# Two-layer graph network on one core: where the first two blocks' row sums are formed, and which engine copies the last values out of PSUM

## The chip, the cores and the metric

The kernel runs on 1 core of one Trainium2 chip. Five engines work side by side, each through its own instructions in order: PE (TensorE, matmuls), DVE (VectorE), ACT (ScalarE), POOL (GpSimd) and SP (SyncE, which here only issues DMAs). The metric is device time in microseconds (us) of one launch; smaller is better.

## What is computed

The reference has two graph-attention layers over N = 4096 nodes with F = 512 features, H = 4 heads of D = 128, all in float32. Cut to what matters here, layer 0 begins like this:

```
h   = relu(layernorm(x))                          # 4096 x 512
Xw  = per head: h_head @ W[head]                  # values, 4096 x 128
f1, f2 = Xw . V[head]                             # two scores for each node
sig = sigmoid(f1[i] + f2[j])                      # per head, 4096 x 4096
att = softmax over j of (adj * sig), where adj != 0
Xa  = att @ Xw                                    # encoder attention
Xn  = batchnorm(Xa) ... MLP ... decoder attention with the same att ... MLP
```

Layer 1 is a second attention of the same kind with other scores. The softmax's denominator is the sum over j of the unnormalised weights; this sum is what the change is about, together with the copying of `Xw`.

## The kernel before, in words

**First phase (L465 to L550).** The nodes are taken in eight blocks `ib` of 512, each of four groups `c` of 128 nodes. For a group, DVE (for the last `c` POOL) normalises the rows (`hn`, L507), PE transposes them (L519), and ACT takes the relu out of PSUM into `hT` (L520). Then, for each of the four groups and for each pair of heads `k`, PE multiplies by the values' weights (L537, 130 columns for each head: 128 values and two scores), ACT copies the 128 values of each head into the large tile `R` (L539), and DVE copies the scores (L540). A PSUM tile holds two heads; the pool `psum` has seven such banks. Meanwhile POOL issues eight DMAs (`copy_adjacency`, L481) that turn the float32 adjacency into bytes, `masks`, in DRAM. The rows of scores go through DRAM (`store_rows`, L189) and come back spread over all partitions (`rowb`).

**Encoder attention (`attention`, L221 to L442).** It runs over eight blocks `n`, each one head and one half of the targets (2048 columns). A block has 32 steps `j`, one for 128 sources. A step makes one weight tile `e` of 128x2048 (`tanh_weights`, L448): ACT computes a tanh (L450) and an exp (L451), DVE multiplies by the mask `a` (L452). PE multiplies the values with the tile into four PSUM banks (L371; for steps 0 and 1 the fourth bank comes later, L368). Every tile must also enter the denominator, and there are three ways:

- by DVE, which adds the tile to `acc` (L392 for the first two tiles of a block, then L394);
- *moved*: POOL issues two DMAs (L386), each for half a tile, that add it to a second sum;
- *by ones*: the tile is held and PE multiplies it with a matrix of ones into the bank `den` (`add_to_den`, L259 to L263). At a block's end the accumulated tiles go into `den` the same way.

The tuples in L62 to L64 say, for each block, which steps are moved and which are by ones: `ENC_FIRST` for block 0, `ENC_SECOND` for block 1, `ENC` for blocks 2 to 7. All steps that are named in neither are added by DVE.

Weight tiles come from eight buffers: two with the tag `ek` (`EP`), six with the name `e`. Mask tiles come from five buffers (`mask_tile`), loaded on SP's queue (L210). Every fifth tile is also kept in DRAM for the decoder by a DMA that ACT issues three steps later (L358). A block's denominators travel at fixed steps of the next block: DVE copies `den` (L268), POOL stores it and loads it as a column (L269, L274), DVE inverts it (L278, L279), POOL stores and spreads it (L282, L287), DVE scales and takes statistics (L561, L564). The raw products are copied out of PSUM by DVE (L557).

The order of instructions on each engine is a scheduler's at build time; `tc.issue_after` (also inside `pinned`) puts chosen instructions behind others on their own engine.

Of the kernel before, what the change touches and what calls it, by code (L numbers as in the profile page):

```python
# [39 lines left out]
N, F, H, D, P = 4096, 512, 4, 128, 128  # L40
IB = 512
NIB = N // IB
# [16 lines left out]
G_MAX = 75.0  # L59


ENC_FIRST = (), (6, 7, 14, 15, 22, 23, 30, 31)  # L62
ENC_SECOND = (13, 15, 17, 20, 22, 25), (5, 6, 10, 11, 30, 31)
ENC = (0, 2, 5, 7, 10, 12, 15, 17, 20, 22, 25), (8, 9, 30, 31)  # L64

GAT_FIRST = (0, 2, 4, 6, 8, 10, 12, 14, 16, 18, 20, 22, 24), (30, 31)
# [19 lines left out]
def kernel(ctx, tc, x, xT, adjT, w0, w0T, v0, wencT, wdecT, vecs, w1, w1T, a1, outT):  # L86
    nc = tc.nc
# [7 lines left out]
    R = [big.tile([P, N], FP, name=f"R{i}") for i in range(5)]  # L95
# [6 lines left out]
    def block(r, j):  # L102
        return r[:, j * D:(j + 1) * D]

    def bank():
        return psum.tile([P, IB], FP, name="ps")

    def bank1():
        return psum1.tile([P, IB], FP, name="den")
# [32 lines left out]
    def scores_of(j, k):  # L142

        return score[:, :, j // (NJ // NTB), 2 * k:2 * k + 2, j % (NJ // NTB)].rearrange("p s h -> p h s")
# [24 lines left out]
    def rsqrt(dst, var, eps):  # L169
        nc.vector.tensor_scalar_add(dst, var, eps)  # L170
        nc.scalar.activation(dst, dst, AF.Sqrt)
        return nc.vector.reciprocal(dst, dst)
# [12 lines left out]
    def heads_of(pv):  # L185

        return pv[:, 0:2 * DX].rearrange("p (h x) -> p h x", x=DX)

    def store_rows(dst, src, queue=nc.scalar):  # L189

        n = src.shape[-1]
        pr = bank()
        nc.tensor.transpose(pr[0:n, 0:P], src, ident)
        fr = consts.tile([P, P], FP, name="fr")
        nc.vector.tensor_copy(fr[0:n, :], pr[0:n, 0:P])
        queue.dma_start(dst.rearrange("h (q p) -> (h q) p", p=P), fr[0:n, :])

    def targets(tb):
        return score[:, 0, tb].rearrange("p h q -> p (h q)")

    def load_row(rowb, d, row):

        return nc.sync.dma_start(rowb, everywhere(d, row, 0, TB))

    def mask_tile(keep):
        return keep.tile([P, TB], U8, name="a", bufs=5)

    def load_mask(a, tb, j):

        return nc.sync.dma_start(a, masks[tb][j // MG][(j % MG) * P:(j % MG + 1) * P, :])  # L210

    @contextmanager
    def pinned(behind):

        with ExitStack() as stack:
            for i in behind:
                stack.enter_context(tc.issue_after(i.ins))
            yield
# [238 lines left out]
    with tc.tile_pool(name="keep", bufs=1) as keep:  # L457

        with tc.tile_pool(name="f_small", bufs=1) as small, tc.tile_pool(name="f_work", bufs=2) as work:
# [18 lines left out]
            def copy_adjacency(n, behind):  # L478

                t, g = divmod(n, NJ // MG)  # L480
                cast = nc.gpsimd.dma_start(masks[t][g], adjT[g * MG * P:(g + 1) * MG * P, t * TB:(t + 1) * TB])  # L481
                tc.add_manual_dep(cast.ins, behind.ins.name,
                                  mybir.DependencyInfo(mybir.DependencyClass.Sync, mybir.DependencyReason.DATA),
                                  reason="others first")

            for ib in range(NIB):
                st = work.tile([P, C, 6], FP, name="st")
                mv = work.tile([P, C, 2], FP, name="mv")
                rstd = work.tile([P, C], FP, name="rstd")

                def deviations(lo, hi):

                    with pinned([first_hn] if ib == 1 or lo == 1 else []):
                        for c in range(lo, hi):
                            nc.vector.bn_stats(st[:, c, :], xs[ib][:, c, :])
                    for c in range(lo, hi):
                        nc.vector.bn_aggr(mv[:, c, :], st[:, c, :])
                    return rsqrt(rstd[:, lo:hi], mv[:, lo:hi, 1], LN_EPS)

                last_dve = deviations(0, 1 if ib == 0 else C)  # L500
                hT = work.tile([P, C, IB], FP, name="hT")
                for c in range(C):
                    if ib == 0 and c == 1:
                        last_dve = deviations(1, C)
                    by_pool = c == C - 1
                    hn = work.tile([P, F], FP, name="hn", tag="hnp" if by_pool else "hn")
                    made = (nc.gpsimd if by_pool else nc.vector).tensor_scalar(  # L507
                        hn, xs[ib][:, c, :], mv[:, c, 0:1], rstd[:, c:c + 1], ALU.subtract, ALU.mult)
                    if ib == 0 and not by_pool:
                        first_hn = made  # L510

                    if by_pool and ib > 0:
                        with tc.issue_after(made.ins):
                            copy_adjacency(ib - 1, half_loaded)
                            if ib == NIB - 1:
                                copy_adjacency(ib, half_loaded)
                    pt = bank().rearrange("p (f n) -> p f n", n=P)
                    for fb in range(C):
                        last_pe = nc.tensor.transpose(pt[:, fb, :], hn[:, fb * P:(fb + 1) * P], ident)  # L519
                    last_act = nc.scalar.activation(hT[:, :, c * P:(c + 1) * P], pt, AF.Relu)  # L520
                if ib == 0:

                    pw = bank1()
                    with tc.issue_after(last_pe.ins):
                        for h in range(H):
                            nc.tensor.matmul(pw[:, 2 * h:2 * h + 2], w0Ts[:, h, :], v0s[:, h, :],
                                             start=True, stop=True)
                    pwh = pw[:, 0:2 * H].rearrange("p (h s) -> p h s", s=2)
                    with tc.issue_after(last_dve.ins):
                        nc.vector.tensor_copy(w0x[:, :, D], pwh[:, :, 0])  # L530
                        nc.vector.tensor_scalar_mul(w0x[:, :, D + 1], pwh[:, :, 1], 0.5)
                for c in range(C):
                    j = ib * C + c
                    for k in range(2):
                        pv = heads_of(bank())
                        for h in range(2):
                            nc.tensor.matmul(pv[:, h, :], hT[:, 2 * k + h, c * P:(c + 1) * P], w0x[:, 2 * k + h, :],  # L537
                                             start=True, stop=True)
                            nc.scalar.copy(block(R[2 * k + h], j), pv[:, h, 0:D])  # L539
                        nc.vector.tensor_copy(scores_of(j, k), pv[:, :, D:DX])  # L540
                if ib == SB - 1:
                    store_rows(rows[0], targets(0))
                    row0 = keep.tile([P, TB], FP, name="rowb", bufs=2)
                    row0_load = load_row(row0, rows[0], 0)
                    with tc.issue_after(row0_load.ins):
                        masks0 = []
                        for j in range(5):
                            a = mask_tile(keep)
                            masks0.append((a, load_mask(a, 0, j)))
# [45 lines left out]
        with tc.tile_pool(name="enc", bufs=1) as spool:  # L595

            with tc.issue_after(last_act.ins), tc.issue_after(masks0[-1][1].ins):
                attention("enc", keep, spool, tanh_weights, R[0:4], lambda h, tb: (rows[tb], h), out_enc,
                          (scaled, statistics), 6, lambda n: (ENC_FIRST, ENC_SECOND, ENC)[min(n, 2)],
                          (TINY, ALU.max), "write", row0=row0, masks0=masks0,  # L600
# [46 lines left out]
        with tc.tile_pool(name="m_small", bufs=1) as small, tc.tile_pool(name="m_work", bufs=3) as work:  # L647
# [10 lines left out]
            for h in range(H):  # L658
# [8 lines left out]
                for ib in range(NIB):  # L667
                    pv = bank().rearrange("p (c d) -> p c d", d=D)
# [40 lines left out]
    with tc.tile_pool(name="l_small", bufs=1) as small, tc.tile_pool(name="l_work", bufs=2) as work:  # L709
# [41 lines left out]
        for fb in range(C):  # L751
            with tc.issue_after(last_pe.ins):
                for h in range(H):
                    k = 2 * (fb * H + h)
# [64 lines left out]
        for ib in range(NIB):  # L819
            for c in range(C):  # L820
# [9 lines left out]
                j = ib * C + c  # L830
                r = rstd[:, c:c + 1]
                pvs, pvs_last = ahead.pop(0) if ahead else values(hT, c)
                for k in range(2):
                    pv = heads_of(pvs[k])
# [143 lines left out]
```

## Time and profile before

| what | us |
|---|---|
| median of 3 runs | 3267.72 (3262.49 to 3267.79) |
| the profiled execution's own time | 3260.23 |
| its span, first to last instruction | 3258.4 |
| PE busy | 3197.5 (98%) |
| DVE busy | 2665.4 (82%) |
| ACT busy | 2601.8 (80%) |
| POOL busy | 477.6 (15%) |

Times inside an execution are counted from the span's start. A row of a group of instructions gives the line, the engine, what it writes and reads, the count, the busy time and the mean of one in ns, then the idle time before it and what ended that. A matmul's record is longer than its share of PE: in float32 each product appears twice in the records, and they overlap. In a stretch without idle time (128 records of L371 in 55.48 us from 253.66 us on) one record takes 0.43 us of PE, and the eight of a step 3.43 us.

The stages, read from the trace: the first phase to about 69 us; encoder block 0 with its first weights at 65 us, block 1 from about 189, block 2 from about 317 (by ACT's work), and the last encoder work at about 1058; then an MLP, the decoder attention, a second MLP, and layer 1.

### The profile page before, as it was taken

How to read it: one execution, taken by the hardware profiler on the slowest of the kernel's cores; microseconds unless marked ns; L12 is line 12 of the kernel's file. 1: busy time of each engine (PE TensorE's matmuls, PEld its weight loads, DVE VectorE, ACT ScalarE, POOL GpSimd, SP SyncE). 2: the span in 40 equal slices, each digit the busy share in tenths (PEclk: the TensorE clock that was granted, in tenths of full speed). 3: DMA queues.
4: the chain of work that ended last, by engine and by line, in shares of the span. 5: the costliest groups of instructions: out<-in, count | busy, mean ns of one | idle time of the engine just before them, and what ended most of it. 6: DMA issues, size and time to landing. Idle time of an engine off the chain costs nothing.

```text
span 3258.4 us, 26085 instructions
## 1 busy us (share of the span) xinstructions
PE 3197.5 (98%) x8723; PEld 1484.0 (46%) x8723; DVE 2665.4 (82%) x1933; ACT 2601.8 (80%) x1908; POOL 477.6 (15%) x622
## 2 busy tenths in 40 slices
PE   7999999999999999999999999999999999999999
PEld 6334434444443464444444444448644444444443
DVE  6999999999999675556655565585599999999998
ACT  7999999999997459899999999566765666666664
POOL 2001221211211000000000000025412222122221
PEclk9999999999999999999999999999999999999999
DMA  9997988988986014434443443231488999889995
GB/s 208 196 195 226 259 227 230 266 224 226 268 232 177 4 64 130 147 127 129 153 142 125 139 153 122 78 121 56 129 207 216 218 229 243 214 210 238 218 214 143
DMA packets 211150, 578.48 MB, mean 178 GB/s; under 512 B 25068, under 2 KB 28172, under 8 KB 195016
## 3 DMA queue, kind: packets, MB, share of 16 engines
q0 software_dynamic: 67968, 222.51, 36.0%
q1 hardware_dynamic: 126432, 293.72, 27.1%
q10 hardware_dynamic: 16616, 60.60, 4.8%
q8 instruction: 68, 1.11, 0.1%
q14 instruction: 66, 0.54, 0.0%
HBM read 377.10 MB, written 84.29 MB: 142 GB/s over the span
## 4 chain that ended last, share of the span: by engine, by line
PE 68%; ACT 12%; DVE 9%; issue 7%; DMA 3%; POOL 0%; ACTq 0%; DVEq 0%; POOLq 0%
PE ps L371 52%; ACT e L450 7%; PE ps L613 7%; DVE e L452 5%; ACT e L451 4%; PE ps L809 3%; DMA a<-mask 2%; DVE acc L394 2%; PE den L262 1%; DVE e L904 1%; DVE R L394 1%; PE ps L670 1%; DMA acc<-e 1%; PE ps L368 1%; PE ps L537 1%
## 5 line engine op out<-in xcount | busy, mean ns | idle before, releaser
L371 PE MATMUL ps<-e,R 128*128 128x512 f32 x6024 | 2614.1, 594 | 37.5 <-DVE e L452 35.2
L371 PEld LDWEIGHTS ps<-e,R 128*128 128x128 f32 x6024 | 1140.1, 190 | 1504.8 <-issue 1396.6
L452 DVE TENSOR_TENSOR e<-e,a 128x2048 f32<-128x2048 f32 (+1 forms) x470 | 1051.7, 2259 | 383.7 <-ACT e L451 369.4
L450 ACT ACTIVATE e<-rowb,score 128x2048 f32<-128x2048 f32 (+1 forms) x470 | 912.4, 1968 | 85.9 <-PE ps L371 43.9
L451 ACT ACTIVATE e<-e 128x2048 f32<-128x2048 f32 (+1 forms) x470 | 870.6, 1879 | 6.1
L903 ACT ACTIVATE e<-rowb,nq,jcol 128x2048 f32<-128x2048 f32 x224 | 461.4, 2090 | 273.7 <-DMA w<-e 133.9
L904 DVE SCALAR_TENSOR_TENSOR e<-e,jcol,a 128x2048 f32<-128x2048 f32 (+1 forms) x265 | 591.8, 2267 | 7.3 <-ACT e L903 7.3
L394 DVE TENSOR_TENSOR acc<-acc,e 128x2048 f32<-128x2048 f32 x130 | 297.1, 2286 | 2.1
L394 DVE TENSOR_TENSOR R<-R,e 128x2048 f32<-128x2048 f32 x123 | 280.5, 2281 | 0.0
L386 POOL DMA_DIRECT2D w<-e x178 | 150.3, 847 | 613.4 <-DMA w<-e 356.1
L613 PE MATMUL ps<-R,w 128*128 128x512 f32 x512 | 220.3, 592 | 0.6 <-DVE w L571 0.6
L386 POOL DMA_DIRECT2D acc<-e x144 | 120.4, 881 | 542.9 <-DMA acc<-e 196.8
L287 POOL DMA_DIRECT2D rb<-rinvs x60 | 34.5, 580 | 1059.2 <-DVE R L561 865.9
L613 PEld LDWEIGHTS ps<-R,w 128*128 128x128 f32 x512 | 97.2, 190 | 122.7 <-issue 117.7
L634 ACT ACTIVATE ex<-ps,bias 128x512 f32<-128x512 f32 x64 | 44.0, 687 | 98.8 <-PE ps L613 79.0
L809 PE MATMUL ps<-w1x,hT 128*128 128x260 f32 x512 | 115.5, 384 | 1.4 <-ACT hT L787 1.4
L809 PEld LDWEIGHTS ps<-w1x,hT 128*128 128x128 f32 x512 | 96.5, 190 | 19.9 <-issue 3.3
L903 ACT ACTIVATE e<-w,nq,jcol 128x2048 f32<-128x2048 f32 (+1 forms) x41 | 67.4, 1711 | 24.5 <-DMA R<-e 24.4
L636 DVE SCALAR_TENSOR_TENSOR ex<-ex,re 128x512 f32<-128x512 f32 x64 | 45.0, 702 | 36.4 <-ACT re L635 36.2
L846 POOL TENSOR_TENSOR vacc<-vacc,R 128x128 f32<-128x128 f32 x120 | 65.8, 576 | 45.3 <-ACT R L839 45.0
L839 ACT ACTIVATE R<-ps,rstd 128x128 f32<-128x128 f32 x128 | 38.5, 371 | 29.3 <-PE ps L809 25.6
L262 PE MATMUL den<-e,ones 128*32 128x512 f32 x424 | 51.1, 598 | 0.0
(172 smaller groups left out, 1246.2 us busy)
## 6 DMA issues: line engine op xcount, KB each, us to landing
a<-mask SPq DMA_DIRECT2D x720, 256.0 KB, 4.1
w<-e POOLq DMA_DIRECT2D x178, 512.0 KB, 6.8
acc<-e POOLq DMA_DIRECT2D x144, 512.0 KB, 6.7
ekeep<-e ACTq DMA_DIRECT2D x48, 1024.0 KB, 7.6
e<-ekeep SPq DMA_DIRECT2D x48, 1024.0 KB, 4.9
mask<-in_adjT POOLq DMA_DIRECT2D x8, 2048.0 KB, 99.4
rowb<-rows SPq DMA_DIRECT2D x16, 1024.0 KB, 7.7
rb<-rinvs POOLq DMA_DIRECT2D x60, 256.0 KB, 4.2
```

The costliest lines, as they stand in the source:

```text
L262: last_ones = nc.tensor.matmul(den[s * 32:(s + 1) * 32, :], ones[:, 0:32], t[:, s * IB:(s + 1) * IB], start=start, stop=stop)
L371: last_main = nc.tensor.matmul(b, block(values[h], j), e[:, s * IB:(s + 1) * IB], start=(j == 0), stop=(j == NJ - 1))
L386: nc.gpsimd.dma_start(into_half, e_half, **({"accum_op": ALU.add} if j > moved[0] else {}))
L394: nc.vector.tensor_add(acc, acc, e)
L450: nc.scalar.activation(e, rowb, AF.Tanh, bias=column(score[:, 1], j, h), scale=0.5)
L451: last_act = nc.scalar.activation(e, e, AF.Exp, scale=0.5)
L452: last_dve = nc.vector.tensor_mul(e, e, a)
L613: last = nc.tensor.matmul(z, w[:, fb, o * P:(o + 1) * P], nodes(src[fb], ib), start=(fb == 0), stop=(fb == C - 1))
L809: m = nc.tensor.matmul(banks[k][:, 0:2 * DX], hT[:, fb, c * P:(c + 1) * P], w1x[:, fb, 2 * k:2 * k + 2, :].rearrange("p h x -> p (h x)"), ...
L846: nc.gpsimd.tensor_add(vacc[:, h, :], vacc[:, h, :], block(v1[h], j))
L903: last_act = nc.scalar.activation(e, rowb, AF.Relu, bias=column(nq, j, h), scale=column(jcol, j, h))
L904: last_dve = nc.vector.scalar_tensor_tensor(e, e, column(jcol2, j, h), a, ALU.add, ALU.mult)
```

## The change

Blocks 0 and 1 each take two more steps by ones. In block 0 the eight steps in four pairs become ten in five pairs, so the pairs also lie at other steps; in block 1 the pair 23, 24 is added. In the first phase the copies of values that ACT made for the last block of nodes (`ib` 7, both heads of a pair: 16 copies) and for the second head of each pair in the block before it (`ib` 6: 8 copies) are made by DVE. Nothing else is touched; the result is the same sum.

```diff
-ENC_FIRST = (), (6, 7, 14, 15, 22, 23, 30, 31)
-ENC_SECOND = (13, 15, 17, 20, 22, 25), (5, 6, 10, 11, 30, 31)
+ENC_FIRST = (), (5, 6, 11, 12, 17, 18, 24, 25, 30, 31)
+ENC_SECOND = (13, 15, 17, 20, 22, 25), (5, 6, 10, 11, 23, 24, 30, 31)
...
                         for h in range(2):
                             nc.tensor.matmul(pv[:, h, :], hT[:, 2 * k + h, c * P:(c + 1) * P], w0x[:, 2 * k + h, :],
                                              start=True, stop=True)
-                            nc.scalar.copy(block(R[2 * k + h], j), pv[:, h, 0:D])
+
+                            by_dve = ib + h >= NIB - 1
+                            (nc.vector.tensor_copy if by_dve else nc.scalar.copy)(block(R[2 * k + h], j), pv[:, h, 0:D])
                         nc.vector.tensor_copy(scores_of(j, k), pv[:, :, D:DX])
```

## The prediction

> **What bounds the kernel now.** The page says PE 98%, but its note says that a busy PE is not at its peak. So I read the waits of ACT alone, from the first weights (64 us) to the start of block 2 (330 us):
>
> ```profile
> engine line waited for: us in total, times, longest us
> ACT e L450 <- DVE e L452: 3.8, 1, 3.8
> ACT e L450 <- DMA acc<-e: 3.2, 1, 3.2
> ACT e L450 <- PE den L262: 1.8, 1, 1.8
> ```
>
> ACT waits three times in 266 us, 8.75 us in all, never in block 0's own steps. Where ACT does not wait, it sets the pace itself. The next view, groups by form between 81 and 330 us, gives the rates (count, busy us, mean ns, idle before):
>
> ```profile
> L452 DVE TENSOR_TENSOR e<-e,a 128x2048 f32<-128x2048 f32 x65 | 146.3, 2284 | 4.8 <-issue 1.7 <-DMA a<-mask 1.6 <-ACT e L451 1.3
> L450 ACT ACTIVATE e<-rowb,score 128x2048 f32<-128x2048 f32 x65 | 126.7, 1988 | 8.7 <-DVE e L452 3.8 <-DMA acc<-e 3.2 <-PE den L262 1.8
> ...
> L394 DVE TENSOR_TENSOR acc<-acc,e 128x2048 f32<-128x2048 f32 x40 | 91.4, 2286 | 0.7
> L262 PE MATMUL den<-e,ones 128*32 128x512 f32 x112 | 13.5, 598 | 0.0
> ```
>
> From start to start an ACT pair (tanh, exp) takes 3.7 us, so 32 steps take 118 us. DVE multiplies at 2.24 us and adds at 2.27: in block 0, 32 x 2.24 + 23 x 2.27 = 124 us. DVE falls behind by 6 us, eight buffers hide that at first, and the bill comes as ACT's waits early in block 1, seen in ACT's timeline (start, us, then idle before it in brackets):
>
> ```profile
> 205.66 2.00 ACT L450 ACTIVATE e<-rowb,score 128x2048 f32<-128x2048 f32 x1 [1.76 <-PE den L262]
> ...
> 222.07 0.35 ACTq L358 DMA_DIRECT2D ekeep<-e  x1
> 222.47 2.00 ACT L450 ACTIVATE e<-rowb,score 128x2048 f32<-128x2048 f32 x1 [3.83 <-DVE e L452]
> ```
>
> The second is the storing DMA in ACT's own queue, which waits for the multiplication of step 4 (ends at 222.0) and holds up step 7. From 330 to 960 us ACT waits 1.8 us, and DVE waits for ACT (21 us between 480 and 970). So ACT carries the encoder to its last block, and what ACT gains by 330 us reaches the end.
>
> [...] before 76 us DVE's score copies idle 12.3 us until ACT's copies. [...] each switch into or out of L262 shows a weight load idle by 0.76 to 0.84 us. [...] mask loads take 15 to 16 us to land between 130 and 210 us, while the adjacency copies run, and 4.5 to 4.8 us just after.
>
> **Part 1: the copies.** ACT loses 16 copies after its last relu. Start to start they fill 63.23 to 64.05, 65.97 to 67.62 and 68.15 to 68.61: 2.93 us, and ACT has no gap there. The 8 copies in block 6 (57 to 61 us) gain nothing: the next relu waits for PE's transposes (0.23 us at 61.00), and PE is nearly full there. DVE takes 24 copies. No row shows 128x128 from PSUM; 64x128 takes 0.27 us (L195), 128x512 takes 0.68 (L557)[...]. I take 0.27: 16 x 0.27 + 8 scores x 0.16 = 5.6 us for block 7, less with overlap, beside DVE's idle 4.29 + 0.85 us between 62 and 68 and 4.08 us of PE. They also spare DVE the wait for ACT. If they stood ahead of the first multiplications, DVE would lose about 1 us; ACT's row DMA (L196) may wait for DVE's copy of the row. So ACT's start moves **2.0 to 2.9 us; I take 2.9**.
>
> **Part 2: block 0.** Two fewer adds: 2 x 2.27 = 4.5 us off DVE. Two more steps by ones on PE: PE's insertion at 107.40 to 109.25 plus 0.52 us of late start is 2.37 us for a pair. PE idles 8.9 us before L371 between 92 and 198 us, so the 2.4 us fit there; with DVE 4.5 us faster about 2 us of idle time are left. No DMA and no instruction of POOL or SP is added or moved. ACT's first two waits (1.76 + 3.83 = 5.6 us) shrink by what DVE gains: the second directly, the first through PE, whose products of steps 30 and 31 idle 1.80 us at 197.46 for DVE before the sums by ones that ACT waits for. But masks land in 15 to 16 us, five buffers allow five steps in flight, and with a pair by ones among five steps DVE asks again after 5 x 2.24 + 3 x 2.27 - 2.3 = 15.7 us. It waited twice, 1.6 us; there are now five such pairs, not four. I take 1.2 us more (0 to 4). **Gain 3.3 us (0.5 to 5.6).**
>
> **Part 3: ACT's third wait.** 3.16 us at 277.73, for the accumulating DMAs of a moved step. POOL issues them behind the spread of the denominators (L287), whose own DMA (L282) waits for DVE's inversion at step 14. All this follows DVE, which moves with ACT by the same amount, so the wait stays: **0**. Bounds: it goes (+3.2), or grows. It grows if the store of denominators lands late: it was issued at 218.31, took 19.4 us and landed as the last adjacency copy did (55.3 + 182.2 = 237.5; same software queue). The column then landed at 243.8. DVE inverts at 253.16, or 246 when 6 to 7 us earlier: 2 us to spare.
>
> **Part 4: block 1 and after.** Two fewer adds, 4.5 us off DVE; one more pair on PE, 2.37 us. PE runs without idle time from 222 to 309 us, so its steps end 2.4 us later by its own clock. The cover is the eight buffers: PE ends step 27 at about 309, ACT reuses that buffer at about 330, 20 us later; a tile that is held for its pair's sum stays one step (3.4 us) longer, which that covers too. Without the cover 2.4 us are lost. After 309 PE idled 3.1 us and then ran eight matmuls at half rate (0.85 us each, 3.4 us more)[...]; these go. POOL's chain in block 2 then starts relatively earlier, and ACT's 1.05 and 0.76 us there on accumulating DMAs shrink: **0.8 us (0 to 1.8).**
>
> **Sum.** 2.9 + 3.3 + 0 + 0.8 = 7.0 us, against the profiled execution's own 3260.23: 3253.2. That execution lies 7.5 us below the median of three, whose runs spread by 5.3; the same gain off the median gives **3260.7**. A measurement tells about 0.2%, 6.5 us, from no change; my sum lies only just beyond.
>
> **The rivals.**
> 1. *The relief is eaten.* Masks set DVE's pace to 237 us, or the inversion waits in DVE's queue for the late column. Only part 1 and some of part 2 remain: 2.9 + 0.5 = 3.4 us, 3264.3. For it: mask loads close to their limit, DMA share 1.05 to 1.06 up to 220 us. Against it: DVE waited for masks only 1.6 us. It decides where masks land later than about 17 us or the copies end after about 240.
> 2. *All waits go.* 2.9 + 8.75 = 11.7, with block 2 at most 13; less what masks take, about 11: 3256.7. For it: DVE becomes nearly as fast as ACT (119.5 against 118 us). Against it: part 3.
> 3. *Slower: PE takes ACT's place.* If the buffers are freed by PE, every added pair is paid: 4 x 1.18 = 4.7 us, and the denominators leave 2.4 us later, so ACT's third wait grows by that; the start's gain is lost in full buffers: +7.1, 3274.8. For it: PE after the change has 32 x 3.43 + 12 = 122 us in block 0, more than ACT's 118. Against: the 20 us above. It decides once PE lags so far that ACT's eighth next tanh finds the buffer taken.
> 4. *Nothing.* The scheduler puts the copies where ACT waits for DVE anyway, and DVE's relief turns into idle time: 3267.
>
> **How the numbers follow.** Forecast (gain 4 to 9.5 us) 0.62; rival 1, 0.12; rival 2, 0.14; rival 3, 0.09; rival 4, 0.03. Above 6.5 us lie rival 2 and some 0.39 of the forecast: faster 0.53. Rival 3 is slower: 0.09. The rest, 0.38, is same. The forecast alone reaches from 3258 to 3264; with rivals 1 and 2, and runs spreading by 5 us, the range is 3253 to 3269, which leaves out rival 3 and the outer ends.
>
> **What would show it.** Right: no ACT copy after the last relu, and the full-size tanh that started at 75.77 near 72.9; 38 adds (L392, L394) in blocks 0 and 1 instead of 42; no wait of ACT near 203 and less than 1 us near 214; a wait for accumulating DMAs near 270; ACT's block 2 about 6 us earlier. Wrong: ACT waits for PE, mask waits of DVE beyond 4 us, the inversion (L278) idle, or that tanh no earlier.

## The result, and the profile after

| kernel | median of ten runs, us | lowest to highest |
|---|---|---|
| before | 3267.64 | 3262.49 to 3273.2 |
| after | 3258.89 | 3255.93 to 3262.7 |

The ratio after to before is 0.998, with a 95% interval of 0.9973 to 0.9988: faster by 6.5 us (3.9 to 8.8). The two medians lie 8.75 us apart, at the far end of that interval. The profiled execution of after took 3257.38 us, its span 3255.6. From the edited copies on, line numbers after are two higher than before (L541 for L539, L542 for L540, L559 for L557, L563 for L561); the lines of the attention are unchanged.

The waits of ACT alone, after, from the first weights to the start of block 2 (line, what it waits for: us in total, times, longest):

```profile
engine line waited for: us in total, times, longest us
ACT e L450 <- DVE e L452: 4.6, 1, 4.6
ACT e L450 <- DVE R L563: 4.0, 1, 4.0
ACT e L450 <- PE den L262: 0.8, 1, 0.8
```

ACT still waits three times, and in all for 9.4 us, where it was 8.75. So blocks 0 and 1 became no shorter for ACT. The row that names L563 is the third wait, which ends at 274.86. DVE's instruction of that line did end then, but an accumulating DMA that POOL had issued at 260.75 landed at 274.76, just as before the one that the prediction names landed at 277.63, 0.10 us ahead of ACT's start at 277.73. So I count it as the same wait for the accumulating DMAs.

```profile
201.22 2.00 ACT L450 ACTIVATE e<-rowb,score 128x2048 f32<-128x2048 f32 x1 [0.85 <-PE den L262]
...
218.41 0.35 ACTq L358 DMA_DIRECT2D ekeep<-e  x1
218.81 3.90 ACT L450 ACTIVATE e<-rowb,score 128x2048 f32<-128x2048 f32 x2 [4.61 <-DVE e L452]
...
274.86 2.00 ACT L450 ACTIVATE e<-rowb,score 128x2048 f32<-128x2048 f32 x1 [3.95 <-DVE R L563]
```

These are lines of ACT's timeline after (start, us; idle before it in brackets). Against 1.76, 3.83 and 3.16 before: the first is smaller, the second and the third are larger (the third was 3.8 us in a second profile of before, e11 below, so its growth says nothing of the change). Why the second did not shrink is in the groups between 81 and 330 us, after (count, busy us, mean ns, idle before):

```profile
L452 DVE TENSOR_TENSOR e<-e,a 128x2048 f32<-128x2048 f32 x65 | 146.5, 2286 | 11.6 <-DMA a<-mask 6.7 <-ACT e L451 4.7
L450 ACT ACTIVATE e<-rowb,score 128x2048 f32<-128x2048 f32 x66 | 128.6, 1988 | 9.4 <-DVE e L452 4.6 <-DVE R L563 4.0 <-PE den L262 0.8
...
L394 DVE TENSOR_TENSOR acc<-acc,e 128x2048 f32<-128x2048 f32 x36 | 82.3, 2286 | 0.6
L262 PE MATMUL den<-e,ones 128*32 128x512 f32 x144 | 17.3, 598 | 0.0
```

DVE has four adds fewer, 36 for 40 and 9.1 us of busy time less, as the change says. But its multiplications now stand idle for 11.6 us where it was 4.8, and 6.7 us of that are for mask tiles. DVE's timeline after shows the three longest of these six waits, all late in block 0 or just behind it:

```profile
157.03 2.29 DVE L452 TENSOR_TENSOR e<-e,a 128x2048 f32<-128x2048 f32 x1 [2.48 <-DMA a<-mask]
...
176.89 2.29 DVE L452 TENSOR_TENSOR e<-e,a 128x2048 f32<-128x2048 f32 x1 [1.02 <-DMA a<-mask]
...
199.89 2.29 DVE L452 TENSOR_TENSOR e<-e,a 128x2048 f32<-128x2048 f32 x1 [1.77 <-DMA a<-mask]
```

So where did 6.5 us come from? ACT's full-size tanhs are the same 462 in every kernel here, in the same order, so the start of the k-th can be compared. The second is an early step of block 0 (the tanh that started at 75.77 before), the 64th begins block 2, the 96th begins block 3, and the 255th is the encoder's last:

| start of the k-th full-size tanh, us | 2nd | 64th | 96th | 255th |
|---|---|---|---|---|
| before | 75.77 | 314.98 | 435.76 | 1026.98 |
| after | 72.25 | 312.09 | 430.85 | 1022.07 |
| gain | 3.52 | 2.89 | 4.91 | 4.91 |

The start gains 3.5 us; blocks 0 and 1 give 0.6 back; block 2 gains 2.0; from there to the encoder's end nothing changes, to a hundredth. The gain arises ahead of block 0 and in block 2; in between, where all the changed steps lie, there is none. The spans of these two profiles differ by 2.8 us only, since after's execution took 2.1 us longer behind the 255th tanh (2233.5 for 2231.4). That part varies in one and the same program: in e11, which is before once more, it took 2234.8.

The start is as it was planned. ACT's timeline after shows tanhs right behind the last relu and no copy; the copies stand in DVE's groups between 55 and 70 us:

```profile
60.98 1.57 ACT L520 ACTIVATE hT<-ps 128x512 f32<-128x512 f32 x3 [0.19 <-PE ps L519]
62.57 1.28 ACT L450 ACT_TABLE_LOAD   x1
...
72.25 3.88 ACT L450 ACTIVATE e<-rowb,score 128x2048 f32<-128x2048 f32 x2
```

```profile
L541 DVE COPY R<-ps 128x128 f32<-128x128 f32 x24 | 6.2, 285 | 3.2 <-PE ps L537 3.2
```

From the end of the last relu (63.36 before, 62.55 after) to that tanh it is 12.41 us before and 9.70 after: 2.71 us gained by the copies. The other 0.81 us lies ahead of the edited place: block 5's values, which no edit touches, were first copied at 51.10 before and at 50.29 after.

### The profile page after: what moved, and what is told of

It reads as the page before. It is cut to its first block, busy times and chain, and to the rows that moved or that the text cites. A ratio compares the mean times of both kernels' runs of the same rounds, so it can differ in the third digit from the quotient of the medians.

```text
span 3255.6 us, 26153 instructions
## 1 busy us (share of the span) xinstructions
PE 3197.0 (98%) x8755; PEld 1483.5 (46%) x8755; DVE 2661.1 (82%) x1953; ACT 2597.9 (80%) x1884; POOL 478.7 (15%) x622
## 4 chain that ended last, share of the span: by engine, by line
PE 67%; DVE 15%; issue 7%; ACT 6%; DMA 5%; POOL 0%; DVEq 0%; ACTq 0%; POOLq 0%
PE ps L371 51%; DVE e L452 9%; PE ps L615 7%; PE ps L811 3%; ACT e L450 3%; DMA a<-mask 3%; DVE acc L394 2%; ACT e L451 2%; DMA acc<-e 1%; PE den L262 1%; DVE R L394 1%; PE ps L672 1%; DVE e L906 1%; PE ps L368 1%; PE ps L537 1%
## 5 line engine op out<-in xcount | busy, mean ns | idle before, releaser
L394 DVE TENSOR_TENSOR acc<-acc,e 128x2048 f32<-128x2048 f32 x126 | 288.1, 2286 | 2.0
L287 POOL DMA_DIRECT2D rb<-rinvs x60 | 34.6, 582 | 1060.8 <-DVE R L563 867.5
```

The lines of the kernel that those rows point to most:

```text
L394: nc.vector.tensor_add(acc, acc, e)
```

## The experiments

**Theory.** The sums by ones in block 0 are worth next to nothing, since the DVE time that they set free becomes waiting for mask tiles. The gain beyond the copies comes from block 1's pair. **Rivals.** ACT's second wait is set by the storing DMA's place in ACT's own queue, not by masks. Or block 0's adds do help, and the gain in block 2 is theirs, carried over.

All ratios below are against before, on the same chip, with 95% intervals; 0.001 is 3.3 us.

### One half of the change at a time (e1, e2)

```diff
 e1: after, with both tuples of before
-ENC_FIRST = (), (5, 6, 11, 12, 17, 18, 24, 25, 30, 31)
-ENC_SECOND = (13, 15, 17, 20, 22, 25), (5, 6, 10, 11, 23, 24, 30, 31)
+ENC_FIRST = (), (6, 7, 14, 15, 22, 23, 30, 31)
+ENC_SECOND = (13, 15, 17, 20, 22, 25), (5, 6, 10, 11, 30, 31)
 e2: the opposite: before, with both tuples of after
```

> Only the 24 copies go to DVE; the sums are those of before. Theory (the early start is what lasts; in block 0 the masks, not the adds, pace DVE): the full-size tanh that started at 75.77 us starts at 72.3, 3.5 us earlier, as in the changed kernel; ACT's three waits after that stay near 1.8, 3.8 and 3.2 us; the encoder ends about 3.5 us earlier than before (last tanh of the four parts near 1031); the time is 3 to 4 us below before, ratio 0.9989. Rival (the sums bring most of it): less than 2 us.

> Only the two tuples change; the copies stay with ACT. Theory: the start stays at 75.8; DVE's waits for masks in blocks 0 and 1 rise from 1.6 (3.3 with the unnamed one) to 6 us or more and eat the 4.5 us of block 0's two adds, so ACT's first three waits keep their sum of 8 to 9 us; only block 2's two waits (1.8 us) go: 1 to 2.5 us below before, ratio 0.9994. Rival (the adds were the bound, as the prediction's second part had it): ACT's first two waits fall from 5.6 to about 2 us, 4 to 5 us below before.

Measured: copies alone 3260.98 us, ratio 0.9992 (0.9984 to 1.0001); sums alone 3261.19, ratio 0.9992 (0.9984 to 1.0). Each point is 2.6 us, and neither alone is certain; together they make 5.2 of the 6.5 us, so the parts add up within their intervals. In its profile e1 missed one expectation: it started 3.2 us earlier than before, but ACT then waited 5.5 us for accumulating DMAs in block 2, and the 255th tanh came at 1028.38, no earlier than before (1026.98). e12 takes that up. In e2 DVE waits for masks as in after, without any edit of the copies:

```profile
DVE e L452 <- ACT e L451: 9.8, 8, 2.9
DVE e L452 <- DMA a<-mask: 7.2, 5, 2.9
```

So it is the sums that make it wait, not the earlier start; e5 and e6 below show that it is those of block 0.

### Six mask tiles, or the store a step later (e3, e4)

```diff
 e3: after, and
-        return keep.tile([P, TB], U8, name="a", bufs=5)
+        return keep.tile([P, TB], U8, name="a", bufs=6)
 with jcol, jcol2 and nq allocated in the pool edge, behind the encoder, for room
 e4: after, and
-                    if j % KEEP == KEEP - 3 and stores:
+                    if j % KEEP == KEEP - 2 and stores:
```

> The changed kernel with six mask tiles instead of five in the encoder and decoder; room comes from three small score tiles that are laid into a later pool. Theory (a mask's latency of 15 to 17 us against five tiles in flight): DVE's waits for masks before 330 us fall from 6.7 to under 1.5 us, ACT's second wait from 4.6 to under 1.5 us, and ACT reaches block 2 some 2 to 4 us earlier than in the changed kernel; 9 to 12 us below before. Rival (the DMA engines can't serve masks faster beside the adjacency copies, so a sixth tile only waits longer): mask waits stay at 5 us or more with landing times near 19 us, and the time is the changed kernel's within 1 us.

> The changed kernel with the storing DMA of a kept tile issued by ACT one step later (four steps after the tile, not three). Theory A (the second wait is only the store's place in ACT's queue): it falls from 4.6 us to about 1, and ACT reaches block 2 up to 3 us earlier. Theory B (DVE's progress sets the pace and the store only shows it): what ACT gains there it loses at the third wait, which grows from 4 to 7 us or so; block 2 starts within 1 us of the changed kernel's.

Measured: e3 3253.37, ratio 0.9971 (0.9961 to 0.9981); e4 3261.3, ratio 0.9992 (0.9984 to 1.0). The waits of ACT, then of DVE, in e3 between 64 and 330 us (lines are three lower than in after: L447 is the tanh, L449 the multiplication):

```profile
ACT e L447 <- DMA acc<-e: 2.9, 1, 2.9
ACT e L447 <- DVE e L449: 1.6, 1, 1.6
```

```profile
DVE e L449 <- ACT e L448: 7.9, 6, 3.1
DVE e L449 <- issue: 1.9, 1, 1.9
DVE e L449 <- DMA a<-mask: 1.3, 2, 0.8
```

With one more mask tile, DVE's mask waits fall from 6.7 to 1.3 us (to 3.2 if the unnamed wait ahead of the same multiplications is counted), ACT's first wait is gone, and its second falls from 4.6 to 1.6. The tile is in use in the decoder too, but behind the 255th tanh e3 takes 2233.5 us, as after does: what it gains lies in the encoder. The rival is right in part: between 170 and 210 us a mask took 19.2 us to land in e3 and 15.3 in after, so that much of the sixth tile's lead was spent on longer landings. In e4 ACT's waits are these:

```profile
ACT e L450 <- DMA acc<-e: 8.4, 1, 8.4
ACT e L450 <- DVE e L452: 2.6, 1, 2.6
ACT e L450 <- PE den L262: 1.9, 1, 1.9
ACT e L451 <- DVE e L452: 0.8, 1, 0.8
```

The second wait shrinks by 2 us, and the first and the third grow by 1.1 and 4.4: what the store's place in the queue held back is paid elsewhere. Block 2 begins at 315.69, later than in after (312.09) and not earlier, so theory A falls. Theory B has the direction; its number, within 1 us, missed too, as blocks 0 and 1 took 2.6 us longer. The store chooses where DVE's lateness shows. In after, masks make a large part of that lateness.

### Block 0's edit and block 1's edit, each left out (e5, e6)

```diff
 e5: after, and
-ENC_FIRST = (), (5, 6, 11, 12, 17, 18, 24, 25, 30, 31)
+ENC_FIRST = (), (6, 7, 14, 15, 22, 23, 30, 31)
 e6: after, and
-ENC_SECOND = (13, 15, 17, 20, 22, 25), (5, 6, 10, 11, 23, 24, 30, 31)
+ENC_SECOND = (13, 15, 17, 20, 22, 25), (5, 6, 10, 11, 30, 31)
```

> The changed kernel without its edit of block 0 (ENC_FIRST as before; copies and block 1's pair kept). Theory (block 0's two adds buy nothing, since masks take their place): ACT reaches block 2's first tanh within 1 us of the changed kernel's 312.1, DVE's mask waits before 330 us fall back to 2 to 4 us, block 2's waits stay at 0 to 1 us, and the time is the changed kernel's within 1 us (ratio to before 0.998 to 0.9985). Rival (block 0's relief still shortens the waits early in block 1): ACT 2 us or more later there, ratio 0.999.

> The changed kernel without block 1's extra pair (copies and block 0's pairs kept). Theory (the pair in block 1 earns its part in block 2, where ACT waits for accumulating DMAs): the start and block 1 as in the changed kernel, but ACT waits for accumulating DMAs in block 2 again, 2 to 5 us, and the encoder ends that much later than the changed kernel's 1029.3; ratio to before 0.999. Rival (block 1's pair does nothing that lasts): block 2 waits under 1 us, ratio 0.998.

Measured: e5, without block 0's edit, 3258.42, ratio 0.9981 (0.9974 to 0.9988), the same as after. e6, without block 1's, 3262.3, ratio 0.999 (0.9983 to 0.9996): half of the gain is gone. These two ran on the same chip, 21 times each, and their medians lie 3.9 us apart. In e5 DVE waits for masks 1.6 us, as before; in e6 6.8 us, as after. In e6 ACT waits in block 2 (330 to 450 us), where after has no wait at all:

```profile
ACT e L450 <- DMA acc<-e: 3.6, 3, 1.9
ACT e L450 <- PE ps L371: 2.9, 1, 2.9
```

The row that names PE is another wait for an accumulating DMA: ACT went on at 392.40, 0.11 us after one had landed. So all 6.5 us are of that kind. In e5, with block 1's pair, there is almost none:

```profile
ACT e L450 <- DMA acc<-e: 0.4, 1, 0.4
```

So the rival that gives block 2's gain to block 0's adds falls: it is block 1's pair.

### The sixth mask tile alone, and with the moved steps (e7, e8, e9)

```diff
 e7: before, with e3's edit
 e8: e3, and
-ENC_SECOND = (13, 15, 17, 20, 22, 25), (5, 6, 10, 11, 23, 24, 30, 31)
+ENC_SECOND = (13, 18, 20, 22, 25, 27), (5, 6, 10, 11, 23, 24, 30, 31)
 e9: e8, with ENC_FIRST of before
```

> The kernel before with six mask tiles alone. Theory (there DVE's adds, not the masks, are the bound in block 0): mask waits before 330 us go from 3.3 us (the unnamed one included) to about 1, ACT's first two waits fall by at most that, 5.6 to 4 or more; 0 to 2.5 us below before. Rival (the sixth mask tile does it all, the adds never mattered): as low as the changed kernel with six masks less its early start, 7 us or more below before.

> The changed kernel with six mask tiles, and block 1's moved steps at 13, 18, 20, 22, 25, 27 instead of 13, 15, 17, 20, 22, 25, so that no moved tile stands behind the spread of the denominators in POOL's queue while ACT needs its buffer. Theory (ACT's third wait is for the tile of step 15, held up behind that spread): the wait of 2.9 us goes to under 0.5 us and block 2 starts 2 to 3 us earlier than the 308.3 of six masks; 12 us or so below before. Rival (DVE's pace alone): the wait moves to a later step of block 1 with about the same size; no gain.

> The kernel of e8 (six mask tiles, moved steps spread) without the change's edit of block 0. Theory (block 0's two adds count as soon as masks come in time): DVE is 3 to 4.5 us later at block 1's step 4, ACT's wait for the store of that step grows from 1.6 to 4 us or more, and block 2's first tanh comes 2 to 4 us later than e8's 305.9. Rival (block 0's edit is worthless with any number of masks): within 1 us of e8.

Measured: e7 3257.82, ratio 0.9976 (0.9967 to 0.9985); e8 3250.09, ratio 0.9954 (0.9942 to 0.9967); e9 3252.93, ratio 0.9962 (0.9949 to 0.9976).

e7 missed its expectation of at most 2.5 us: one mask tile gives the kernel before 7.8 us, as much as the whole change (the intervals overlap). Mask tiles were a limit already, though DVE's waits for them showed only 1.6 us, 3.3 with the unnamed one. ACT's waits in e7:

```profile
ACT e L447 <- DVE e L449: 3.5, 1, 3.5
ACT e L447 <- DMA acc<-e: 2.7, 1, 2.7
```

The wait for `den` (1.8 us) is gone, and block 2 has none. The second wait stays at 3.5 us, though DVE no longer waits for any mask: between 81 and 330 us it idles only 0.9 us before its multiplications, so here its own work, 40 adds of 2.29 us (L391) among it, makes it late. Behind the 255th tanh e7 takes 2231.5 us, as before does (2231.4), so no gain comes from the decoder.

e8 is faster than both kernels, by 15 us against before. Its waits of ACT are two, and none is for an accumulating DMA:

```profile
ACT e L447 <- DVE e L449: 1.6, 1, 1.6
ACT e L448 <- DVE e L449: 1.5, 1, 1.5
```

In after POOL issues the moved tile of step 15 behind the denominators' spread (L287):

```profile
258.58 1.63 POOL L287 DMA_DIRECT2D rb<-rinvs  x3 [5.71 <-DMA rinvs<-dcol]
260.18 1.89 POOL L386 DMA_DIRECT2D acc<-e  x2
```

The later of these two accumulating DMAs lands at 274.76, and ACT goes on at 274.86. With steps 18 and 27 moved in place of 15 and 17, that third wait goes. In e9 block 0's edit is left out again: 1.5 us slower at the 255th tanh (1017.30 against 1015.83), of which only 0.5 us lies in blocks 0 and 1, and the intervals overlap. Block 2 begins 0.3 us later, where 2 to 4 were expected. With six mask tiles block 0's edit does what it was made for: ACT's second wait is 3.5 us in e9 and 1.6 in e8. But e8 pays 1.5 us of it back in a new wait at 270.65, the second row above. So even with masks in time the edit is a small thing.

### Lighter adjacency copies (e10)

```diff
-                cast = nc.gpsimd.dma_start(masks[t][g], adjT[g * MG * P:(g + 1) * MG * P, t * TB:(t + 1) * TB])
+                cast = nc.gpsimd.dma_start(masks[t][g], masks[0][g] if t else adjT[g * MG * P:(g + 1) * MG * P, t * TB:(t + 1) * TB])
```

> The changed kernel, with five mask tiles, but the second half of the masks is not made from the adjacency: it is copied from the first half's bytes, a quarter of the traffic read, so the graph's second half of targets is not computed from its own adjacency. Theory (the adjacency copies on the same DMA engines make a mask take 15 to 19 us): the copies end by 150 us instead of 240, masks asked for after that land in 4 to 9 us, DVE's mask waits before 330 us fall from 6.7 to under 3 us, ACT's second wait from 4.6 to under 1.5 us, and block 2's first tanh comes 3 us or more earlier than 312. Rival (masks are late for another reason, such as SP's queue or the load's own size): mask waits stay above 5 us.

Measured: 3283.09, ratio 1.0053 (1.0039 to 1.0067), slower, and no clean test. A copy out of `masks` waited 22.71 us for an earlier copy, and held up what stands behind it in POOL's queue, the normalised rows of the last group of nodes. POOL's timeline, ACT's longest wait and DVE's waits for masks in e10:

```profile
72.95 0.54 POOL L481 DMA_DIRECT2D mask<-mask  x1 [22.71 <-DMA mask<-in_adjT]
73.54 2.07 POOL L507 TENSOR_SCALAR hn<-R,mv,rstd 128x512 f32<-128x512 f32 x1
```

```profile
ACT hT L520 <- PE ps L519: 14.2, 1, 14.2
```

```profile
DVE e L452 <- DMA a<-mask: 15.7, 2, 8.0
```

The expectation of under 3 us of mask waits missed by far. Both waits end by 146.50 us, and the last copy landed at 146.33. While the copies of bytes ran, masks took long to land, 23.2 us in the median between 90 and 130 us; after them DVE waited for no mask up to 330 us. That is what can be read. Mask loads issued between 130 and 170 us landed after these times (kilobytes each, median us to landing), first in before, then in after, then in e10:

```profile
a<-mask SPq DMA_DIRECT2D x11, 256.0 KB, 16.5
```

```profile
a<-mask SPq DMA_DIRECT2D x10, 256.0 KB, 19.4
```

```profile
a<-mask SPq DMA_DIRECT2D x7, 256.0 KB, 2.6
```

The same load takes 2.6 us once no adjacency copy runs beside it; between 170 and 210 us the DMA engines' mean busy share is 0.37 in e10 and 1.06 in after. How the engines divide themselves between copies and loads is not seen in these figures. What e10 says of the second wait (3.1 us) can't be separated from its late start.

### Before and the copies again (e11, e12)

```diff
 e11: before, unchanged
 e12: e1, unchanged
```

> The kernel before once more, unchanged, for its profile alone: how much the waits differ between executions. The profiled execution of before was 7 us below the median of its runs. Theory (block 2's waits for accumulating DMAs vary from execution to execution, and the one shown was a lucky one): 3 to 7 us there instead of 1.8, the first three waits again 8 to 9 us, and a span of 3262 or more. Rival (the spread lies elsewhere, in the decoder or layer 1): block 2 waits 1 to 2.5 us again.

> The kernel of e1 (copies alone) once more, for its profile alone. In e1's profile ACT waited 5.5 us in block 2, and the early start was gone by the encoder's end. Theory (that is one draw of the same spread as in before): block 2 waits anywhere from 1.5 to 6 us, and the encoder ends earlier than before's by 2.7 us less the difference. Rival (the early start itself makes block 2 wait): 5 us or more again.

Measured: e11 3265.62, e12 3260.9, each one execution with its profile. They ask how far one profile of block 2 can be trusted. The waits of ACT from 330 to 450 us in before, in e11 and in e12:

```profile
ACT e L450 <- DMA acc<-e: 1.8, 2, 1.1
```

```profile
ACT e L450 <- DMA acc<-e: 4.5, 3, 2.6
```

```profile
ACT e L450 <- DMA acc<-e: 3.8, 2, 2.4
```

The very same program waited 1.8 us in one execution and 4.5 in the other. The prediction had only the first. e11's rival is right as well: its span is 5.4 us longer than that of before, and only 2.0 of these lie in the encoder; 3.4 lie behind the 255th tanh. In e12 the wait is 3.8 us, so the 5.5 of e1 was in part a draw. Still, the two profiles of the copies alone reach the 255th tanh only 0.8 us ahead of the two of before (1027.1 against 1028.0 in the mean), though they started 2.7 us ahead. Whether the early start itself lengthens block 2 without block 1's pair can't be told from two profiles each.

### All profiles side by side

"Blocks 0 and 1" is the time from the 2nd to the 64th full-size tanh, "block 2" from the 64th to the 96th. "Spread" is how long after the 64th tanh POOL issued the spread of block 1's denominators (the three DMAs of L287, L284 with six mask tiles). One execution each, us; "b0" and "b1" are the edits of the two tuples.

| kernel | 2nd tanh | blocks 0 and 1 | spread | block 2 |
|---|---|---|---|---|
| before | 75.77 | 239.21 | 54.5 | 120.78 |
| e11 before again | 74.24 | 239.92 | 54.4 | 123.56 |
| e1 copies | 72.60 | 240.02 | 55.1 | 124.54 |
| e12 copies again | 72.05 | 239.65 | 55.1 | 122.96 |
| e6 copies, b0 | 72.32 | 239.38 | 56.1 | 125.71 |
| e5 copies, b1 | 72.43 | 239.20 | 52.6 | 119.26 |
| e2 b0, b1 | 75.86 | 239.99 | 52.5 | 118.86 |
| after: copies, b0, b1 | 72.25 | 239.84 | 52.2 | 118.76 |
| e4 after, store later | 73.26 | 242.43 | 57.6 | 119.81 |
| e7 six masks | 75.30 | 236.51 | 49.6 | 118.75 |
| e3 after, six masks | 73.47 | 234.85 | 44.9 | 118.75 |
| e9 e8 without b0 | 72.39 | 233.71 | 50.0 | 118.76 |
| e8 six masks, moved | 72.62 | 233.23 | 50.8 | 118.75 |

e10, with its late start, is left out. From the 96th to the 255th tanh all take 591.2 us, but for e9 (592.4) and e4 (595.3); otherwise these three stages hold the whole difference in the encoder. In none of them is block 2 shorter than 118.75 us, called its floor here. Whether it is reached goes with the spread: with up to 52.6 us block 2 is within 0.5 us of the floor, from 54.4 us on 2.0 to 7.0 above. Only e4, whose ACT queue has another order, stands off this rule. It is a threshold and no line: with 54.4 to 55.1 us block 2 lies anywhere from 2.0 to 5.8 above the floor. Block 1's pair brings the spread forward by 2.0 us (e2 against before) to 3.9 (after against e6), the sixth mask tile by 4.9 (e7 against before), and e7 reaches the floor without block 1's pair. The traces show the way from the one to the other. Right behind the spread POOL issues the next moved tile, in two DMAs, and ACT needs that tile's buffer about 67 us after the 64th tanh (in e11 it waits from 67.2 on). With block 1's pair or the sixth mask tile the second of these DMAs has landed by then: at 64.3 us in after, 64.9 in e2, 63.9 in e5, 62.8 in e7. In e11, e1 and e6 it lands at 69.7, 69.5 and 70.2, and ACT goes on 0.1 us after that, with a further wait for the moved tiles behind it. This is also where one program differs from itself: before and e11 both issue this DMA at 56.6 us, but it takes 9.4 us in before, and comes in time, and 13.1 in e11. No run moves POOL's chain alone.

## Why the prediction was right in its total and wrong in its parts

**The total.** 7.0 us less were forecast, 6.5 (3.9 to 8.8) were measured. As shown below, that agreement is in good part luck.

**Part 1, copies: right.** 2.9 us forecast; 2.71 between the two profiles, and 2.69 between the mean 2nd tanh of the nine profiles with the copies (72.60) and of the four without (75.29). A 128x128 copy out of PSUM took DVE 0.285 us, forecast 0.27. (The trace of before did have one such copy, at L195: 0.28 us.) That the eight copies in block 6 gain nothing is in agreement, but was not tried alone.

**Part 2, block 0: wrong.** 3.3 us forecast. In blocks 0 and 1, b0 shortens e6 against e1 and e12 by 0.6 and 0.3 us (239.38 for 240.02 and 239.65), and lengthens after against e5 by 0.6 (239.84 for 239.20): nothing, within 0.6 us. The ratios of after and e5 differ by 0.0001. Fewer adds and other places of the pairs come together in this edit, and no run parts them. The term that failed is the one for mask tiles, "I take 1.2 us more (0 to 4)": between the two profiles of before and after the named mask waits rose by 5.1 us (1.6 to 6.7), or by 3.4 if the 1.7 us of "issue" ahead of the same multiplications is counted with before's. The period of 15.7 us in which DVE asks again was set against landings of 15 to 16 us, those of the kernel before; between 130 and 170 us the median was 16.5 before and 19.4 after. As an estimate, which leaves out the time that a multiplication holds its tile, five tiles in 19.4 us are one in 3.9, slower than ACT's pair at 3.7; six in e3's 19.5 are one in 3.3. And since the stall falls late in block 0, just ahead of ACT's waits, it came out of the very lateness that the adds had saved. The second wait, which was to fall under 1 us, grew to 4.6. This is rival 1, "the relief is eaten", in its place and near the threshold that the prediction gave (landings beyond 17 us); its total (3264.3) did not come, as block 1 gave more, and of its other half, the late column, nothing came: it was loaded at 240.22 and inverted at 249.50 without idle time.

**Part 3: right in kind.** The wait for the accumulating DMAs stayed, at 4.0 us for 3.2; the kernel before itself showed 3.8 in e11. e8 bears out its cause, the moved tile behind the spread in POOL's queue.

**Part 4, block 1: right mechanism, size too small.** "0.8 us (0 to 1.8)" was taken from one execution whose waits in block 2 were 1.8 us. The five profiles without b1 lie 2.0 to 7.0 us above the floor, 4.8 in the mean; the four with it and five mask tiles 0 to 1.1, 0.4 in the mean. So b1 is worth 4.3 us on the mean, five times the forecast; the medians of e5 and e6 lie 3.9 apart. What varies from execution to execution is how long one accumulating DMA takes (9.4 and 13.1 us above); why, no run shows. Two details of this part were misread. In the stretch at half rate after 309 us (granted clock 0.50 between 318 and 320 us) three matmul records started 0.85 us apart and two more 0.58 and 0.70 us, not eight at 0.85; it cost about 1.7 us, not 3.4. And PE's idle time there did not go: it was 3.1 us before and is 2.1 after, at 311.50 and 316.49; the stretch at half rate is gone (granted clock 1.00), and no run shows what brought it on.

**The sum as it was**, from these means: 2.7 for the copies, about nothing for block 0, about 4.3 for block 1, together 7.0. One term too large and one too small had nearly cancelled out, by luck.

**The rivals.** "All waits go" fell: ACT waits 9.4 us. "PE takes ACT's place" fell: in blocks 0 to 2 of after no wait of ACT is for the release of a tile by PE, and the one for `den` got shorter. One of the prediction's signs of being wrong did come, mask waits beyond 4 us, and two signs of being right stayed away: ACT still waits near 203 us (0.85 us, at 201.22), and 4.6 us near 214 instead of less than 1. Block 2 "about 6 us earlier" was 2.9 at its start and 4.9 at its end.

## What to carry to other kernels

Before an engine is relieved, look at what feeds it. As an estimate, n tiles in flight that take L to land allow n steps in L: here five in 19.4 us, one in 3.9. The kernel before waited only 1.6 us for masks, and a sixth tile still gave it 7.8 us. L itself grew with n here: with the sixth tile it went from 15.3 to 19.2 us between 170 and 210 us. Ask what one more tile would do before shifting work; here it gave as much as the shift, and the two together with block 1's moved steps at other places 15 us. And a wait of a later stage should be sized from more than one execution: the same program showed 1.8 and 4.5 us.

## What was not expected of the hardware

A 256 KB load took 19.4 us to land beside the casting copies (median in after, 130 to 170 us) and 2.6 us without them (e10, 170 to 210 us), with the queue that it was issued on unchanged. And one program's block 2 took 120.78 us in one execution and 123.56 in another, while the six hundred us after it agreed within 0.03 us; behind the encoder the same two executions differed again, by 3.4 us. In block 2 an accumulating DMA that both issued at the same time after the 64th tanh took 9.4 us in the one and 13.1 in the other.
